# Where the first image's sampling starts in a conv-attention-MLP kernel, the queue of the feed-forward's row loads, and the order of the attention's pools

## The chip, the cores and the metric

The kernel runs on one core of a Trainium2 chip. The engines are TensorE (PE), VectorE (DVE), ScalarE (ACT), GpSimd (POOL) and SyncE (SP, which here only issues DMAs); ACT and POOL issue DMAs too, each in the order of its own instruction stream. Working data lies in SBUF (128 partitions), matmul results in PSUM. The metric is the device time of one execution in microseconds, taken as the median over several executions; lower is better.

## The reference

The input is four images of 64 x 64 positions with 256 channels in 32-bit floats, and everything stays in that type. Two layers follow each other. Cut to what matters:

```python
# layer 0, per image; xn is the group-normalised image
xp = xn @ in_w + in_b
x1 = silu(batchnorm(depthwise_conv3x3(xn)))
offset = x1 @ off_w + off_b                  # 8 groups x 9 points x (x, y), per position
mask = softmax(x1 @ mask_w + mask_b)         # over the 9 points
out = sum over the 9 points of mask * bilinear_sample(pad(xp), grid + offset)
x = x + (out @ out_w + out_b)
# layer 1, per image of 4096 tokens; t = x
n1 = layernorm(t); q = n1 @ Wt; k = n1 @ Wx.T
a = softmax_over_k( tanh(q[:, None] + k[None, :] + bh) @ Wa + ba )      # 32 units
t = t + a @ n1
n2 = layernorm(t); w = n2 @ wr + br
idx = the 2047 tokens with the largest w
t = t + scatter(idx, (gelu(n2[idx] @ w1 + b1) @ w2 + b2) * w[idx]) + n2
```

## The kernel before, in words

**Offsets and weights.** `offsets_and_weights` is a generator over four images of eight slabs each (a slab is 512 tokens, four tiles of 128). Each slab normalises, convolves on PE and DVE, makes offsets and masks, and turns them into weights over a 5 x 5 window of the projected image; these go to DRAM (`wt`), the projected image as well (`xp`), and a table of it for gathers (`tab`). In each slab it can yield at five places, so that other work is put between: before its window, after the first step of the window, and after three more.

**Sampling.** `sample_image(n)` is a generator too. Offsets beyond the window are rare; `list_tokens` makes a list of the tokens that have one, with a chain of small DVE operations and 32 PE matmuls of one-hot columns (L647 to L651), and `exact_rows` computes those tokens exactly with 144 indirect gathers `ga` on POOL (L724). For all others the window sum runs in four chunks of 1024 tokens, two channel halves and 25 window positions: load `wb` (the weight of that position, broadcast over channels, L819), multiply it with the shifted image `xs` (L828), and add to the accumulator `ac` (L838). Each of the two DVE operations is 128 x 1024 elements, and there is a yield behind each. A finished chunk goes through PE (L784) and is written to `t` in DRAM. At its end the exact rows are put over the approximate ones (L762).

**First stage.** All four images' offsets come first, with the sampling of image 0 beside them. In the driver (near L1522) the generator of offsets runs alone through image 0, and then each yield of the 24 slabs of images 1 to 3 is followed by 4, 4, 4, 3 and 3 steps of the sampler, 18 a slab.

**Per image.** The driver then loops over the images. A first scope holds the feed-forward of the image before, the preparation of this image's attention (layer norm, unit products, exponentials to `kf` and through DRAM to `qf`) and steps of the next image's sampling; a string of turns sets the order. A second scope holds the attention with sampling beside it: PE forms `d` from `qf` and `kf` (L1017), ACT takes logarithms into a ring of buffers `r` (pool `rp`, L1111), POOL, DVE and PE multiply them up, and exponentials `et` (pool `ep`) weight the values. The last feed-forward runs alone.

**Feed-forward.** `feed_forward` finds the threshold of the 2047 largest weights, writes each of 32 tiles of rows with an indirect scatter on POOL to its sorted place in DRAM (`sort`, L1423), and then loads four chunks of 512 sorted rows back (`chunk`, L1455, on SP's queue). Each load waits for all 32 scatters. ACT normalises the rows (L1463), PE transposes them (L903), and the two matmuls with gelu follow (`ph` L1483, `py` L1489); the results are scattered to the output on POOL (L1496). `chunk(s + 1)` is called behind the second of the four scatters of chunk s.

**Order.** A planner (the Tile framework) orders each engine's instructions; those wrapped in `keep` or issued through `pinned` stay in program order on their engine, others may be moved. SBUF pools are a stack: a scope's pools take their bytes in the order in which they are named, and a pool that lies on bytes of a closed one waits for all that used the closed pool. In the first scope of an image the order is `one` (53 KB per partition: the feed-forward's buffer `big` and its weights), `two`, `sb`, `row`, `rp`. In the attention it is `two`, `sb` (15 KB together), `rp` (24 KB), `qp` (16 KB, the queries `qf` and `qn`), `ep` (34 KB), `ap`.

Of the kernel before, what the change touches and what calls it, by code (L numbers as in the profile page):

```python
# [18 lines left out]
NB, H, W, C = 4, 64, 64, 256  # L19
L = H * W  # L20
NT = L // P
# [8 lines left out]
SLAB = 8  # L30
# [7 lines left out]
PVB = 8  # L38
# [8 lines left out]
def layers_kernel(ctx: ExitStack, tc: tile.TileContext, a, out: bass.AP):  # L47
    nc = tc.nc
# [183 lines left out]

    S = SimpleNamespace(bank=True, wants=False, gather=True, left=0, tables=[])

    def bank_taken():
        S.wants = not S.bank
# [28 lines left out]
    def offsets_and_weights(images, slab, rows_bufs):  # L267
# [300 lines left out]
        ns = NT // slab  # L568
# [4 lines left out]
        for i in range(len(images) * ns):  # L573
            at, s = divmod(i, ns)
            if s == 0:
                cur = ahead
                after = front(images[at + 1]) if at + 1 < len(images) else {}
            one, two, three, four = after.get(s, nothing)
            cur.taps(s)
            one()  # L580
            if s + 1 < ns:
                cur.convolution(s + 1)
            elif at + 1 < len(images):
                ahead = image(at + 1)
                ahead.convolution(0)
            if at:
                yield
            window = cur.window(s)
            three()
            next(window)  # L590
            if at:
                yield
            two()
            if s % 2 == 0:
                rows16 = cur.projection(s // 2)
                next(rows16)
            else:
                next(rows16, None)
            if last:
                last[0].turn(last[1])  # L600
            last = cur, s
            for _ in range(3):
                next(window)
                if at:
                    yield
            four()
            if at == 0 and s == ns - 1:
                yield
        last[0].turn(last[1])

    def positions(fl, vec):
# [154 lines left out]
    def sample_image(n, sums=1):  # L766

        S.left = STEPS
        uf = yield from list_tokens(n)
        yield
        exact = []
        single = exact_rows(n, uf, exact)

        def matmuls(c, ac, i):
            g = c * (CH // P) + i
            xr = S.sb.tile([P, 2, C], F32, tag="xr", name="xr")
            nc.sync.dma_start(out=xr, in_=x_d[n, g * P : (g + 2) * P].rearrange("(t p) c -> p t c", p=P))  # L780
            pm = S.ps_m.tile([P, 2, C], F32, tag="pm", name="pmo")
            for j in range(2):
                for k in range(CC):
                    nc.tensor.matmul(  # L784
                        pm[:, j, :], ac[:, k, rows(i + j)], outwp[:, k, :],
                        start=(k == 0), stop=(k == CC - 1),
                    )
            keep(nc.gpsimd.tensor_add(  # L788
                xr, xr, outb.rearrange("p (o c) -> p o c", o=1).to_broadcast([P, 2, C])
            ))  # L790

            def add():
                (nc.vector if sums == 1 else pinned).tensor_add(xr, pm, xr)
                nc.sync.dma_start(
                    out=t_d[n][g * P : (g + 2) * P].rearrange("(t p) c -> p t c", p=P), in_=xr
                )

            return add

        late, adds = [], []  # L800

        def outputs():

            while adds:
                adds.pop(0)()
            for _ in range(min(2, len(late))):
                adds.append(late.pop(0)())

        for c in range(L // CH):
            ac = S.dn.tile([P, CC, CH], F32, tag="ac", name="ac", bufs=sums)  # L810
            for f in range(CC):
                xs = S.dn.tile([P, CH // W + 4, MP], F32, tag="xs2", name="xs2")
                o = c * (CH // W) * MP
                nc.sync.dma_start(
                    out=xs.rearrange("p r w -> p (r w)"), in_=xp_d[n][f, :, o : o + (CH // W + 4) * MP]
                )
                for d in range(ND):
                    wb = S.dn.tile([P, CH], F32, tag="wb", name="wb", bufs=2)
                    nc.sync.dma_start(  # L819
                        out=wb, in_=wt_d[n][f, d : GH * ND : ND, c * CH : (c + 1) * CH].partition_broadcast(CG)  # L820
                    )
                    src = xs[:, d % WIN : d % WIN + CH // W, d // WIN : d // WIN + W]
                    if d == 0:
                        pr = ac[:, f, :]
                    else:
                        prt = S.dn.tile([P, CH], F32, tag="prd", name="prd")
                        pr = prt
                    keep(nc.vector.tensor_tensor(  # L828
                        pr.rearrange("p (r w) -> p r w", w=W), src, wb.rearrange("p (r w) -> p r w", w=W),
                        ALU.mult,  # L830
                    ))
                    S.left -= 1
                    if d % 8 == 2:
                        outputs()
                    own = S.gather and next(single, None)
                    yield
                    if d > 0:
                        keep(nc.vector.tensor_add(ac[:, f, :], ac[:, f, :], pr))  # L838
                        S.left -= 1
                        yield  # L840
                    while own:
                        own = next(single, None)
                        S.left -= 1
                        yield
            if sums > 1:
                late = [functools.partial(matmuls, c, ac, i) for i in range(0, CH // P, 2)]
                continue
            for i in range(0, CH // P, 2):
                while bank_taken():
                    yield  # L850
                matmuls(c, ac, i)()
                S.left -= 1
                yield
        while late or adds:
            outputs()
            yield
        for _ in single:
            S.left -= 1
            yield
        put_rows(n, *exact[0])  # L860
        S.left = 0
# [505 lines left out]
    def feed_forward(n, vec):  # L1367
# [40 lines left out]
        sl, _ = positions(eq, vec)  # L1408
# [3 lines left out]
        sl, _ = positions(gt, vec)  # L1412
# [36 lines left out]
        def chunk(s):  # L1449

            o = nh + s % 2 * nx
            xs = big[:, o : o + nx].rearrange("p (t c) -> p t c", t=4)
            o = nh + 2 * nx + s % 2 * nv
            vs = big[:, o : o + nv].rearrange("p (t c) -> p t c", t=4)
            get = nc.sync.dma_start(  # L1455
                out=xs, in_=sort_d[n][s * 512 : (s + 1) * 512].rearrange("(t p) c -> p t c", p=P)
            )
            for ins in put:
                tc.add_manual_dep(get.ins, ins.name, in_order, reason="rows in order")
            si = S.two.tile([P, 4], I32, tag="si", name="si")  # L1460
            vec.tensor_scalar(si, xs[:, :, C + 3], float(n * L), None, ALU.add)
            for t in range(4):
                nc.scalar.activation(  # L1463
                    vs[:, t, :], xs[:, t, :C], AF.Identity, bias=xs[:, t, C + 1 : C + 2], scale=xs[:, t, C : C + 1]
                )
            xT = S.row.tile([P, CC, 512], F32, tag="vT", name="xT")
            transpose4(xT, vs, vec)

            nc.gpsimd.tensor_tensor(vs, vs, xs[:, :, :C], ALU.add)
            for t in range(4):  # L1470
                vec.scalar_tensor_tensor(
                    vs[:, t, :], b2, xs[:, t, C + 2 : C + 3], vs[:, t, :], ALU.mult, ALU.add
                )
            held[s] = xs, vs, si, xT
# [43 lines left out]
    with scope(  # L1518
        ("a_one", 1, 0), ("a_xn", 2, 0), ("a_ld", 2, 0), ("a_wk", 2, 0), ("a_w1p", 1, 0), ("a_sm", 2, 0),
        ("smp", 2, 0), ("two", 2, 0), ("sb", 2, 0), ("dn", 1, 0), ("a_t", 3, 1), ("a_m", 3, 1), ("ps_m", 2, 1),  # L1520
    ):
        others = offsets_and_weights(range(NB), SLAB // 2, 1)  # L1522
        next(others)
        first = sample_image(0, 2)
        for at, _ in enumerate(others):
            for _ in range((4, 4, 4, 3, 3)[at % 5]):
                next(first, None)
        for _ in first:
            pass
    sample_any(0)  # L1530
    for n in range(NB):
        with scope(("att", 1, 0), ("smp", 2, 0), ("dn", 1, 0)):
# [24 lines left out]
                        pass  # L1557
            S.gather = True
            with scope(
                ("two", 2, 0), ("sb", 2, 0), ("rp", 6, 0), ("qp", 2, 0),  # L1560
                ("ep", 2 * PVB + 1, 0), ("ap", 1, 0), ("ps_d", 2, 1), ("ps_n", 3, 1), ("ps_m", 1, 1),
            ):
                attention(n, v, kf, [sampling])
        attention_any(n)
# [41 lines left out]
```

## Time and profile before

| | us |
|---|---|
| median of three executions | 10425.71 (10424.51 to 10445.72) |
| the profiled execution, its span | 10430.83, 10429.1 |
| PE, DVE, ACT, POOL busy in the span | 9290.6, 8530.2, 7464.3, 5220.7 |
| first stage: offsets of all images beside sampling of image 0 | 0 to 1361 |
| preparation and attention of image 0 | 1361 to 1470, to 3465 |
| feed-forward 0 with preparation 1, attention 1 | 3465 to 3850, to 5765 |
| feed-forward 1 with preparation 2, attention 2 | 5765 to 6150, to 8060 |
| feed-forward 2 with preparation 3, attention 3 | 8060 to 8373, to 10130 |
| feed-forward 3, alone | 10130 to 10429 |

The boundaries are read from the starts of token loads, query loads and last matmuls on the timeline. Shares of the whole span say little here: attention, which the change touches only at its start, is three quarters of it. So the stretches in question are cut out by their start and end, and the busy and idle time of each engine in a stretch is compared with the stretch. A timeline line gives start, duration, engine, source line, operation, tile written from tiles read, shape, count, and in brackets the idle time of the engine before it with what ended that.

### The profile page before, as it was taken

What the parts mean: (1) busy time and instruction counts of PE and PEld (TensorE: products, weight loads), DVE (VectorE), ACT (ScalarE), POOL (GpSimd) and SP (SyncE); (2) the same over time, 40 slices, a digit from 0 to 9 for tenths busy, and PEclk for the clock granted to TensorE, in tenths of its full rate; (3) what the DMA queues carried; (4) which work ended last, traced back from release to release, by engine and by line L of the source; (5) the groups of instructions that cost most, each with busy time, mean ns of one, the idle gap of its engine ahead of it and who ended that gap; (6) DMA issues with size and microseconds to landing.
All of it is one profiled execution on the core that took longest, in us unless ns stands there. A gap on an engine that the chain in (4) does not pass through costs nothing. (4 is left out here: it accounts for less than half of the span.)

```text
span 10429.1 us, 117382 instructions
## 1 busy us (share of the span) xinstructions
PE 9290.6 (89%) x38892; PEld 4512.6 (43%) x38892; DVE 8530.2 (82%) x13743; ACT 7464.3 (72%) x8525; POOL 5220.7 (50%) x3042
## 2 busy tenths in 40 slices
PE   5777779999999589999999589999999699999995
PEld 3444434444444344444444344444444344444443
DVE  5788979898989679899898689899898367777772
ACT  3333348887888438888888358888887389999991
POOL 0231027776555327676655247677555155555552
PEclk8788879999999789999999789999999799999997
DMA  3466642222222342112111442122111300000002
GB/s 104 137 200 192 200 129 64 62 65 60 72 66 72 121 151 54 52 53 56 53 58 44 139 137 54 53 51 56 52 58 38 103 13 8 10 7 7 7 5 76
DMA packets 381591, 766.07 MB, mean 73 GB/s; under 512 B 49360, under 2 KB 212848, under 8 KB 380944
## 3 DMA queue, kind: packets, MB, share of 16 engines
q1 hardware_dynamic: 290448, 608.84, 18.3%
q0 software_dynamic: 30144, 45.87, 3.0%
q10 hardware_dynamic: 60352, 103.50, 2.8%
q8 instruction: 312, 5.11, 0.2%
q14 instruction: 335, 2.74, 0.1%
HBM read 580.88 MB, written 177.14 MB: 73 GB/s over the span
## 5 line engine op out<-in xcount | busy, mean ns | idle before, releaser
L1032 DVE TENSOR_TENSOR r<-nn,r 128x512 f32<-128x512 f32 x6144 | 3942.2, 683 | 865.7 <-PE nn L1027 807.4
L1027 PE MATMUL nn<-qn,kf 32*128 32x512 f32 (+1 forms) x12288 | 4518.4, 640 | 134.5 <-DVE r L1032 97.5
L1117 POOL TENSOR_TENSOR r<-r 128x1024 f32<-128x1024 f32 x1024 | 2708.2, 2645 | 2645.1 <-DVE r L1032 2633.0
L1111 ACT ACTIVATE r<-d 128x1024 f32<-128x1024 f32 x3072 | 3114.2, 1014 | 1093.4 <-DVE r L1121 688.8
L1017 PE MATMUL d<-qf,kf 32*128 32x512 f32 (+1 forms) x12288 | 3338.7, 632 | 77.3 <-DMA qf<-qf 42.9
L1113 ACT ACTIVATE r<-r 128x1024 f32<-128x1024 f32 x3072 | 3124.1, 1051 | 32.7
L1027 PEld LDWEIGHTS nn<-qn,kf 32*128 32x128 f32 (+1 forms) x12288 | 1400.3, 185 | 1900.0 <-DVE r L1032 1452.4
L1055 PE MATMUL pv<-v,et 128*128 128x257 f32 x8192 | 2110.6, 401 | 14.9 <-DVE acv L1079 14.9
L1055 PEld LDWEIGHTS pv<-v,et 128*128 128x128 f32 x8192 | 1511.6, 194 | 979.0 <-issue 770.7
L1017 PEld LDWEIGHTS d<-qf,kf 32*128 32x128 f32 (+1 forms) x12288 | 1017.7, 186 | 1340.0 <-issue 734.0
L1119 POOL TENSOR_TENSOR r<-r 128x512 f32<-128x512 f32 x1024 | 1330.5, 1299 | 98.3 <-DVE r L1032 23.1
L828 DVE TENSOR_TENSOR prd<-xs,wb 128x1024 f32<-128x1024 f32 x768 | 983.6, 1281 | 79.2 <-DMA wb<-wt 71.4
L838 DVE TENSOR_TENSOR ac<-ac,prd 128x1024 f32<-128x1024 f32 x768 | 990.9, 1290 | 6.6
L724 POOL DMA_INDIRECT ga<-tab,tii x576 | 698.6, 1213 | 353.8 <-DVE so L738 208.6
L1039 ACT ACTIVATE et<-et,nshift 128x512 f32<-128x512 f32 x1024 | 723.5, 707 | 29.7 <-DVE et L1124 29.7
L1121 DVE TENSOR_TENSOR r<-r 128x512 f32<-128x512 f32 x1024 | 720.3, 703 | 4.1 <-POOL r L1117 3.7
L1124 DVE TENSOR_TENSOR et<-r 128x512 f32<-128x512 f32 x1024 | 697.4, 681 | 0.4
L263 PE MATMUL pc<-xn,diag 128*128 128x512 f32 x1008 | 452.2, 604 | 21.7 <-ACT xn L397 8.3
L788 POOL TENSOR_TENSOR xr<-xr,outb 128x512 f32<-128x512 f32 x64 | 88.1, 1381 | 551.4 <-DMA xr<-in_x_dram 486.1
L263 PE MATMUL ptc<-ident,xp 128*128 128x128 f32 (+1 forms) x576 | 136.9, 352 | 207.3 <-ACT tb L456 204.9
L263 PEld LDWEIGHTS pc<-xn,diag 128*128 128x128 f32 x1008 | 191.7, 193 | 257.2 <-issue 223.6
L456 ACT COPY tb<-ptc 128x256 f32<-128x256 f32 (+1 forms) x288 | 104.5, 370 | 240.7 <-PE ptc L263 132.4
(342 smaller groups left out, 5251.9 us busy)
## 6 DMA issues: line engine op xcount, KB each, us to landing
wb<-wt SPq DMA_DIRECT2D x800, 512.0 KB
tab<-tb ACTq DMA_DIRECT2D x128, 256.0 KB
v<-t SPq DMA_DIRECT2D x64, 512.0 KB
xs<-xp SPq DMA_DIRECT2D x32, 680.0 KB
xp<-xp ACTq DMA_DIRECT2D x32, 544.0 KB
xt<-in_x_dram SPq DMA_DIRECT2D x32, 512.0 KB
xr<-in_x_dram SPq DMA_DIRECT2D x64, 256.0 KB
t<-xr SPq DMA_DIRECT2D x64, 256.0 KB
```

What stands on the lines that cost most here:

```text
L263: return lambda *args, **kw: keep(op(*args, **kw))
L828: keep(nc.vector.tensor_tensor(pr.rearrange("p (r w) -> p r w", w=W), src, wb.rearrange("p (r w) -> p r w", w=W), ALU.mult,))
L838: keep(nc.vector.tensor_add(ac[:, f, :], ac[:, f, :], pr))
L1017: keep(nc.tensor.matmul(d[:, j, :], kf[g, blk, rows(kt)], qs[q][0][g, blk, :], start=True, stop=True))
L1027: keep(nc.tensor.matmul(nn, kf[g, blk, rows(kt)], qs[q][1][g, blk, :], start=True, stop=True))
L1032: keep(nc.vector.tensor_tensor(r[:, j, :], ns[j], r[:, j, :], ALU.mult))
L1039: keep(nc.scalar.activation(ets[b], ets[b], AF.Exp, bias=nshift))
L1055: keep(nc.tensor.matmul(pv, ets[b0 + i][:, rows(j)], v[:, k0 + i, :], start=(i == 0), stop=(i == PVB - 1)))
L1111: keep(nc.scalar.activation(rs[b, p], ds.pop((b, p)), AF.Ln))
L1113: keep(nc.scalar.activation(rs[b, p], rs[b, p], AF.Exp, scale=-1.0))
L1117: keep(nc.gpsimd.tensor_tensor(rs[b, 1], rs[b, 1], rs[b, 2], ALU.add))
L1119: keep(nc.gpsimd.tensor_tensor(rs[b, 1][:, 0], rs[b, 1][:, 0], rs[b, 3][:, 0], ALU.add))
```

## The change

Several things are changed. The generator of offsets yields from the fifth slab of the first image on (it yielded only from the second image on), and yields its slab number, 0 to 31. The driver puts 3, 3, 2, 2 and 2 steps of the sampler into slabs 4 to 7 and 4, 4, 3, 3 and 3 into each later one. The list of far tokens, which needs the offsets of the whole image, is made by the sampler at its first multiply at or after slab 9 and no longer as its first act; later images list first, as before. The four row loads of a feed-forward go from SP's queue to POOL's. In the attention's scope `ep` takes the place of `rp` and `qp`, behind it come `rp`, `ap` and `qp`.

```diff
-    S = SimpleNamespace(bank=True, wants=False, gather=True, left=0, tables=[])
+    S = SimpleNamespace(bank=True, wants=False, gather=True, left=0, tables=[], listing=True)
...
-            if at:
-                yield
+            if i >= ns // 2:
+                yield i
             window = cur.window(s)
             three()
             next(window)
-            if at:
-                yield
+            if i >= ns // 2:
+                yield i
...
             for _ in range(3):
                 next(window)
-                if at:
-                    yield
+                if i >= ns // 2:
+                    yield i
             four()
-            if at == 0 and s == ns - 1:
-                yield
...
         S.left = STEPS
-        uf = yield from list_tokens(n)
-        yield
-        exact = []
-        single = exact_rows(n, uf, exact)
+        exact, single = [], None
+        if S.listing:
+            uf = yield from list_tokens(n)
+            yield
+            single = exact_rows(n, uf, exact)
...
                     if d % 8 == 2:
                         outputs()
+                    if single is None and S.listing:
+                        uf = yield from list_tokens(n)
+                        yield
+                        single = exact_rows(n, uf, exact)
                     own = S.gather and next(single, None)
...
-            get = nc.sync.dma_start(
+            get = nc.gpsimd.dma_start(
                 out=xs, in_=sort_d[n][s * 512 : (s + 1) * 512].rearrange("(t p) c -> p t c", p=P)
             )
...
-        others = offsets_and_weights(range(NB), SLAB // 2, 1)
-        next(others)
+        slabs = NT * 2 // SLAB
+        S.listing = S.gather = False
         first = sample_image(0, 2)
-        for at, _ in enumerate(others):
-            for _ in range((4, 4, 4, 3, 3)[at % 5]):
+        for at, i in enumerate(offsets_and_weights(range(NB), SLAB // 2, 1)):
+            if i == slabs + 1:
+                S.listing = S.gather = True
+
+            for _ in range((3, 3, 2, 2, 2)[at % 5] if i < slabs else (4, 4, 3, 3, 3)[at % 5]):
                 next(first, None)
...
-                ("two", 2, 0), ("sb", 2, 0), ("rp", 6, 0), ("qp", 2, 0),
-                ("ep", 2 * PVB + 1, 0), ("ap", 1, 0), ("ps_d", 2, 1), ("ps_n", 3, 1), ("ps_m", 1, 1),
+                ("two", 2, 0), ("sb", 2, 0), ("ep", 2 * PVB + 1, 0), ("rp", 6, 0), ("ap", 1, 0), ("qp", 2, 0),
+                ("ps_d", 2, 1), ("ps_n", 3, 1), ("ps_m", 1, 1),
```

## The prediction

> **What bounds the kernel now.** The page's 40 slices come first. PE holds 9 in the long attention stretches; the first three and a half slices (the offsets of all images beside the first image's sampling) are lower on PE and higher on DVE.
>
> ```profile
> PE   5777779999999589999999589999999699999995
> DVE  5788979898989679899898689899898367777772
> PEclk8788879999999789999999789999999799999997
> ```
>
> The change touches that first stage, three overlaps of a feed-forward with the next attention's preparation, and the last feed-forward. Next I cut the first stage at the window-weight clears that open slabs 4, 7, 8 and 31, and asked each stretch for its busy time. Columns: window, length, then busy us and count for PE, PE loads, DVE, ACT, POOL, then clock, DMA share, GB/s.
>
> ```profile
> 251.90:335.70 83.80, 64.67 (x210) 40.14 (x209) 54.88 (x115) 45.70 (x71) 1.14 (x8) 0.82 0.28 100
> 335.70:403.10 67.40, 54.67 (x194) 35.84 (x193) 34.25 (x101) 18.11 (x29) 7.74 (x8) 0.77 0.25 71
> 403.10:1338.40 935.30, 699.95 (x2170) 395.33 (x2168) 849.59 (x1163) 321.69 (x541) 175.63 (x161) 0.84 0.63 197
> 1338.40:1361.50 23.10, 13.13 (x60) 10.45 (x60) 12.69 (x26) 4.84 (x12) 3.82 (x3) 0.72 0.42 133
> ```
>
> Slabs 8 to 30 take 935.3/23 = 40.67 us each and DVE is busy for 849.59 of 935.30: DVE bounds them, with 85.7/23 = 3.7 us idle a slab. Slabs 4 to 6 take 27.9 us each with DVE idle for 28.9 us in all, and the step from slab 7 to slab 8 leaves it idle for another 33.1. Tile by tile, the sampling is an equal pair of DVE operations that begins only there, although its operands were loaded long before:
>
> ```profile
> L828 DVE TENSOR_TENSOR prd<-xs,wb x206: 1160/1224/3487, 399.2 to 1496.5; 128x1024 f32<-128x1024 f32 x103
> L838 DVE TENSOR_TENSOR ac<-ac,prd x205: 1159/1224/2299, 400.5 to 1483.2; 128x1024 f32<-128x1024 f32 x103
> L819 SPq DMA_DIRECT2D wb<-wt x217: 512/513/619, 212.3 to 1498.8; - x109
> ```
>
> The last lines are from the timeline (start, duration, engine, line, in brackets the idle time before and who ended it). At 381 us DVE makes the list of far tokens and stands 15.1 us for PE's matmuls of it. At 3589 to 3631 the row loads of the first feed-forward stand at the head of SP's queue until the scatters have landed; wb loads for the sampling stand behind them.
>
> ```profile
> 381.22 0.87 DVE L647 TENSOR_TENSOR oh<-slotr,bf 128x256 f32<-128x256 f32 x2 [15.08 <-PE pl L651]
> ...
> 3605.48 1.22 DVE L838 TENSOR_TENSOR ac<-ac,prd 128x1024 f32<-128x1024 f32 x1
> ...
> 3623.01 0.96 POOL L1423 DMA_INDIRECT sort<-v,rif  x1 [0.30 <-DMA sort<-v,rif]
> 3625.77 0.37 SPq L1455 DMA_DIRECT2D big<-sort  x1
> 3626.25 0.52 SPq L819 DMA_DIRECT2D wb<-wt  x1
> ...
> 3629.41 2.07 ACT L1463 ACTIVATE big<-big 128x256 f32<-128x256 f32 x4 [25.10 <-DMA big<-sort]
> 3631.11 1.23 DVE L828 TENSOR_TENSOR prd<-xs,wb 128x1024 f32<-128x1024 f32 x1 [24.41 <-DMA wb<-wt]
> ```
>
> Durations are from one execution of 10430.8 us (span 10429.1), 5.1 above the median of 10425.7; savings are taken off the median.
>
> **Part A, the sampling begun in slab 4.** Nothing is removed: 48 steps of the sampler (four slabs of 3+3+2+2+2) move into slabs 4 to 7, and later slabs take 17 steps instead of 18. A step is one DVE operation of 1.22 us, so 48 x 1.23 = 59 us of DVE work arrives where DVE was idle for 28.9 + 33.1 = 62.0 us. Not all the idle time can be filled. Slabs 4 to 6 become DVE bound: 54.88/3 = 18.3 us of own work plus 12 x 1.23 = 14.8, plus the 3.7 us that such a slab leaves idle, is 36.8 instead of 27.9. They lengthen by 27 us in all, and the sampling that leaves slabs 8 onward pays it back. I count the stage by DVE's idle time, since its busy time, 951.4 us from 251.9 to 1361.5, stays. Idle before: 28.9 + 33.1 + 85.7 + 10.4 (the tail after 1338.4) = 158.2. After: slabs 4 to 6, 3 x 3.7 = 11; the step from 7 to 8, 10 (its 33.1 less the list's 15.1 and less a part that samples fill); slabs 8 to 30 the same 85.7; the list, now in slab 9 among full DVE work, 12 (its 15.1 with a little in front of it); the tail 10.4. Sum 129, a gain of 29 us. The list's own DVE and PE work is moved only. Bounds: nothing, if the first image's chain through PE and ACT lengthens by as much as is inserted; 47, if the list hides entirely and slab 7 is as tight as the others (158.2 - 4 x 3.7 - 85.7 - 10.4). Moved DMAs: 48 steps carry some 25 wb loads of 0.51 us on SP and the xs loads, which in before sit prefetched from 212.3 on; in slabs 4 to 7 the DMA share is 0.25 to 0.28 against 0.63 later, so they are hidden. The 144 gathers on POOL move later by about a slab; POOL is busy for 176 of 935 us and hides them. With 408 + 48 steps against about 423 the sampler ends in slab 30 instead of 31, so its closing matmuls and row writes overlap the last windows; this is inside the 10.4 of tail.
>
> **Part B, the order of pools in the attention.** SBUF is a stack; a new pool waits for everything that used its bytes. The query buffers lay on the feed-forward's bytes and move to bytes that are free early; the exponent ring of six (rp) instead moves onto the feed-forward's, the preparation's small pool (two) and its row pool. At the third transition the queries wait for the last scatter:
>
> ```profile
> 8373.24 1.22 SPq L1000 DMA_DIRECT2D qf<-qf  x2
> ...
> 8379.59 1.94 ACT L1111 ACTIVATE r<-d 128x1024 f32<-128x1024 f32 x2 [28.84 <-PE d L1017]
> ```
>
> ACT writes rp there, so the earliest start is when the scatter has landed, 8373.3: a gain of 6.3 us. At the first two transitions rp would wait instead for the last reader of `two`, the cast of `wide` on DVE (3856.58, behind a wait of 16.8 us for rows of x), while the first Ln ran at 3854.37: a loss of 2.3, and 2.0 by the same rows of the second. Net gain 2; bounds -4 (no gain at the third) and +18 (the cast does not hold rp, and all three start with the scatter's landing, at the first 3848.2 against 3854.37).
>
> **Part C, row loads on POOL's queue.** Removed: 16 loads at 0.36 to 0.58 us of SP. Added: 16 on POOL. SP no longer stands from 3596 to 3625, so wb loads go on; but DVE keeps program order and has only some seven operations (8 us) before the minimum over PE's product at 3638.8, which needs ACT's exponent, and ACT itself stands for the rows until 3629. Gain 0 to 8 at each of two overlaps (the third has no sampling), taken 4: 8 us. Cost: the trace has no plain load on POOL. One indirect scatter of 128 rows takes 0.96 us: as one instruction the load would cost as much, by count of its 512 rows 3.8. Against SP's 0.46 the first load of a feed-forward, on its path, costs 0.5 to 3.4 us more; I take 2 (no row favours an end) at each of four: 8. The other twelve cost nothing, because chunk 2's rows land by 10334.2 and are first used by PE's transposes near 10349.8; without that cover they cost 4 to 7 each (rival 2). What is queued behind a waiting load on POOL is the next chunk's addition, 2.35 us, which waits for the same rows anyway. Net 0, bounds -14 (0 less 4 x 3.4) to +14 (16 less 4 x 0.5).
>
> The Trainium skill, "SBUF — State Buffer", section "SBUF: two separate sides", speaks against part C: GpSimd writes descriptors itself and can be held up while DVE runs certain fast copies, about 620 against 3100 ns. By that the four first loads could cost about 2.5 us more each, 10 in all. The scatters here took 0.96 us while DVE stood and up to 1.96 beside its work, so the trace shows the direction and less of the size.
>
> Sum: 29 + 2 + 0 = 31; 10425.7 - 31 = 10395 (10400 on the profiled execution's own time).
>
> **Rivals.**
> 1. The first image is a chain. Slabs 4 to 7 lengthen by what is inserted, and only the list changes place: A is 0, time 10424. For it: PE is busy for 64.7 of 83.8 us there and waits for ACT. Against: 62 us of DVE idle.
> 2. Slower, by one mechanism: POOL's stream keeps each next chunk's load where the code has it, behind the chunk's second scatter. That scatter ends at 10324.6 in the last feed-forward; landing 2.4 (the shortest of the row DMAs), ACT 2.1, transposes 2.8 and copy 1.2 give xT at 10333.1 or later, where PE began the next chunk at 10329.1: 4 us, or 7 with a 3.8 us load, for each of 12 chunks, 48 to 84. Taken 60: 10455. It decides from 31/12 = 2.6 us a chunk. Against it: the SP loads of chunks 0 and 1 go out together, and on POOL chunk 1's addition (3687.23) stands ahead of chunk 0's first scatter (3694.39), so the planner does move such work ahead of code order.
> 3. C pays fully: ACT's order shifts too and both overlaps gain their whole 24.4 and 25.4 us, 42 more than counted: 10353. Against it: ACT waits for the rows themselves.
>
> **How the numbers follow.** Forecast .50 (own range 10378 to 10414: A between 47 and 10), rival 1 .17, rival 2 .20, rival 3 .13. Leaving out the outer part of rivals 2 and 3 gives 10362 to 10450. A measurement tells about 0.2%, 20.9 us, from no change: below 10404.8 lies most of the forecast and rival 3, .55; between lies rival 1 and a part of the forecast and of 2, .25; above 10446.6 most of rival 2 and some unknown, .20.
>
> **What would show it.** Right: sampling on DVE from about 255 us; slabs 4 to 6 near 37 us; a list stall near 450; the stage's token loads at about 1330; at 3590 no wb wait of 24 us but a wait for PE or ACT; loads on POOL's queue beside the first scatters landing; the first Ln of image 3 some 6 us sooner after the last scatter. Wrong: slabs 8 to 30 still at 40.7 us with the stage's end unmoved, or chunks of the last feed-forward further apart than the 28.4 us of now.

## The result and the profile after

The changed kernel takes 10424.3 us against 10440.1 us for the kernel before, run beside it: a ratio of 0.9987 (95% interval 0.9980 to 0.9993), some 14 us less (7 to 21). The forecast was 31 us less. By the bound of 0.2% this is the case "within", which had been given a chance of 25%. The forecast was counted from a median of 10425.7, which the longer series puts at 10440. So the raw time lies outside the forecast's own range (10378 to 10414) and inside the wide one (10362 to 10450), and it meets the 10424 of rival 1 by luck: 14 us off the old median would be some 10412. The profiled execution of the changed kernel took 10422.3 us (span 10420.5).

The stages, each from one profiled execution. "Overlap" is a feed-forward with the next attention's preparation, from its first token load to the first logarithm of the attention.

| stage, us | before | after | difference | forecast |
|---|---|---|---|---|
| first stage, to its token load | 1361.5 | 1344.3 | -17.2 | -29 |
| preparation 0 | 109.8 | 110.2 | +0.4 | 0 |
| overlap 1 | 360.7 | 371.1 | +10.4 | +2 by B, -2 by C |
| overlap 2 | 362.6 | 375.0 | +12.4 | +2 by B, -2 by C |
| overlap 3 | 288.5 | 283.0 | -5.5 | -6 by B, +2 by C |
| attentions 0 to 3, sum | 7714.2 | 7705.7 | -8.5 | 0 |
| last feed-forward | 231.9 | 231.2 | -0.7 | +2 |

The first stage, in the same view as before (window, length, busy us and count of PE, PE loads, DVE, ACT, POOL, then clock, DMA share, GB/s). The windows are slabs 4 to 6, the step from 7 to 8, slabs 8 to 28, and slabs 29 to 31:

```profile
258.24:367.39 109.15, 74.71 (x239) 44.27 (x237) 97.40 (x153) 48.33 (x74) 1.16 (x8) 0.81 0.48 163
367.39:404.25 36.86, 31.09 (x107) 18.50 (x107) 33.18 (x66) 13.87 (x24) 0.00 (x0) 0.86 0.59 189
404.25:1255.30 851.05, 668.43 (x2093) 386.58 (x2091) 752.94 (x1085) 302.74 (x502) 183.48 (x168) 0.84 0.63 193
1255.30:1344.30 89.00, 55.09 (x190) 36.19 (x190) 50.21 (x94) 26.94 (x52) 3.50 (x3) 0.75 0.32 109
```

The same last three slabs of the kernel before:

```profile
1264.90:1361.50 96.60, 52.85 (x186) 34.24 (x184) 82.38 (x121) 22.94 (x46) 3.82 (x3) 0.75 0.51 168
```

Slabs 4 to 6 now take 36.4 us each and slab 7 takes 36.9 instead of 67.4: the sampler fills them as forecast. But DVE, idle for 14.2 of the last 96.6 us before, is idle for 38.8 of the last 89.0 after. The sampler has run out of work in slab 29, and the last offsets stand alone as a chain again. Much of the idle time was moved from the beginning of the stage to its end.

The whole stage in the same columns, before and after:

```profile
0.00:1361.50 1361.50, 973.56 (x3094) 568.07 (x3094) 1098.04 (x1750) 477.32 (x787) 203.53 (x229) 0.83 0.53 166
0.00:1344.30 1344.30, 972.54 (x3094) 572.71 (x3094) 1087.49 (x1750) 480.31 (x788) 203.35 (x229) 0.83 0.54 168
```

DVE runs the same 1750 instructions. It is idle for 263.5 us before and 256.8 after, so only 6.7 of the 17.2 us are idle time; its busy time fell by 10.5.

In the sampling's tiles, the multiply begins at 249.6 instead of 399.2:

```profile
L827 DVE TENSOR_TENSOR prd<-xs,wb x207: 1159/1224/2300, 249.6 to 1493.7; 128x1024 f32<-128x1024 f32 x104
L841 DVE TENSOR_TENSOR ac<-ac,prd x207: 1160/1224/2174, 250.9 to 1499.1; 128x1024 f32<-128x1024 f32 x104
```

Then the timeline of the first overlap after the change (start, duration, engine, line, operation, and in brackets the idle time before and who ended it):

```profile
3584.84 1.22 DVE L827 TENSOR_TENSOR prd<-xs,wb 128x1024 f32<-128x1024 f32 x1
...
3602.99 1.60 POOL L1458 DMA_DIRECT2D big<-sort  x2 [2.18 <-DMA sort<-v,rif]
...
3607.15 2.08 ACT L1466 ACTIVATE big<-big 128x256 f32<-128x256 f32 x4 [33.53 <-DMA big<-sort]
...
3610.18 3.78 PE L953 MATMUL pk<-mm,sel 64*128 64x512 f32 x4 [32.03 <-ACT qe L961]
...
3615.05 1.23 DVE L263 TENSOR_REDUCE least<-pk 128x1 f32<-128x1024 f32 x1 [28.99 <-ACT kf L954]
```

No wait for window weights of 24 us is left, as forecast. DVE went on for seven more operations, to 3586, and then stood 29.0 us for the unit's exponential; PE stood 32.0 us where it had stood 20.6, and ACT 33.5 where it had stood 25.1. One long stall on DVE was exchanged for another. PE's line before:

```profile
3633.14 2.89 PE L950 MATMUL pk<-mm,sel 64*128 64x512 f32 x3 [20.58 <-DVE mm L263]
```

The transitions, with the last output scatter, the cast of `wide` and the first logarithm. First overlap, then third:

```profile
3820.98 2.57 POOL L1499 DMA_INDIRECT out_dram<-big,si  x1 [4.49 <-DMA out_dram<-big,si]
...
3839.50 0.14 DVE L263 CAST wide<-lo 1x1 int32<-1x1 f32 x1
...
3839.88 1.94 ACT L1114 ACTIVATE r<-d 128x1024 f32<-128x1024 f32 x2 [58.62 <-DMA tr<-t]
...
8357.58 2.55 POOL L1499 DMA_INDIRECT out_dram<-big,si  x1 [2.40 <-DVE lo L263]
...
8368.70 1.94 ACT L1114 ACTIVATE r<-d 128x1024 f32<-128x1024 f32 x2 [23.01 <-DMA out_dram<-big,si]
```

The same before, first overlap and then the third's last scatter (its logarithm, at 8379.59, stands in the prediction):

```profile
3837.95 2.55 POOL L1496 DMA_INDIRECT out_dram<-big,si  x1 [4.43 <-DMA out_dram<-big,si]
...
3854.37 1.94 ACT L1111 ACTIVATE r<-d 128x1024 f32<-128x1024 f32 x2 [53.47 <-PE d L1017]
...
3856.58 0.14 DVE L263 CAST wide<-lo 1x1 int32<-1x1 f32 x1
...
8361.67 2.55 POOL L1496 DMA_INDIRECT out_dram<-big,si  x1 [2.52 <-DVE lsm L263]
```

From scatter to logarithm it takes 18.9 us at the first (16.4 before), where the logarithm now follows the end of the cast by 0.2 us, and 11.1 us at the third (17.9 before). In all seven executions with the new order of pools the logarithm follows the cast's end by 0.2 to 0.5 us at the first two transitions; in all four with the old order it starts 1.6 to 2.9 us ahead of the cast's end.

### The profile page after: what moved, and what is told of

It reads as the page before. It is cut to its first block, busy times and chain, and to the rows that moved or that the text cites. A ratio compares the mean times of both kernels' runs of the same rounds, so it can differ in the third digit from the quotient of the medians.

```text
span 10420.5 us, 117367 instructions
## 1 busy us (share of the span) xinstructions
PE 9281.3 (89%) x38892; PEld 4511.9 (43%) x38892; DVE 8523.7 (82%) x13743; ACT 7466.9 (72%) x8526; POOL 5246.2 (50%) x3058
## 3 DMA queue, kind: packets, MB, share of 16 engines
q1 hardware_dynamic: 282000, 600.32, 17.8%
## 5 line engine op out<-in xcount | busy, mean ns | idle before, releaser
L1426 POOL DMA_INDIRECT sort<-v,rif x128 | 133.2, 1040 | 291.6 <-DVE rif L263 176.2
```

## The experiments

After this reading I held that part A gives 17 us and loses the rest at the stage's end, and that part C costs some 10 us in each of the first two overlaps. The first four runs test both, and a way to make C pay. Ratios are against the kernel before, with their 95% intervals.

### e1: row loads back on SP

```diff
-            get = nc.gpsimd.dma_start(
+            get = nc.sync.dma_start(
```

> The changed kernel with the row loads back on SP's queue. Stages are measured from the first token load of an overlap (feed-forward with the next preparation) to the first logarithm of its attention: 360.8, 362.6 and 288.5 us before, 371.1, 375.0 and 283.0 changed. My theory: part C makes the first two longer, by 4 us of later rows (the 32 scatters take 45.4 instead of 42.2 us beside more DVE work) and 4 us of matmuls at half clock behind a longer PE stall. Then both return to about 361 to 364, the third stays at 283, and the time falls by some 20 us. Rival: the pool order (part B) or the sampler's other position (part A) makes them longer. Then they stay at 371 to 375 and the time stays.

Measured: ratio 0.9989 (0.9980 to 0.9999), 10431 us. The overlaps took 370.8, 363.4 and 282.5 us. The second fell by 11.6, the first not at all, and the time did not fall. The 20 us expected did not come.

### e2: only the row loads on POOL

```diff
# in the kernel before
-            get = nc.sync.dma_start(
+            get = nc.gpsimd.dma_start(
```

> The kernel before with the row loads on POOL's queue and nothing else changed. My theory: the first two overlaps go from 360.8 and 362.6 to about 369 and 373, the third and the last feed-forward stay within 1 us, the first stage ends at 1361 as before; the time rises by 15 to 20 us. Rival (parts A and B cause the longer overlaps): 361 and 363, no change of time.

Measured: ratio 1.0006 (0.9996 to 1.0016), 6 us more with an interval that holds zero. Overlaps 368.2, 364.7 and 292.9 us. The third, where no change was expected, rose by 4.4. With e1 this says that C costs between nothing and some 10 us in all. My theory of 20 us finds no support: it had been read from one pair of executions.

### e0: the changed kernel again

> The changed kernel once more, beside the runs that follow. First token load at 1344 to 1352, overlaps (first token load to first logarithm) 371 and 372 plus or minus 5, 283 plus or minus 5 for the third. If the length of a preparation is set by how many of its matmuls run at half clock, about 0.5 us each, the spread between executions of the same code follows that count; the rival, that it is fixed by the code, expects the same length again within 1 us.

Measured: ratio 0.9992 (0.9983 to 1.0001). First token load 1338.1, 6 us earlier than the expected 1344 to 1352; overlaps 366.9, 367.8 and 283.0 us, so 4 and 7 us shorter than in the first execution of the same code. The preparation of image 0, which no part of the change edits, shows what varies. Three executions of it, of e2, of the changed kernel and of e3:

```profile
1360.60:1467.20 106.60, 74.90 (x238) 39.71 (x238) 80.88 (x185) 36.84 (x54) 4.87 (x5) 0.79 0.52 173
```

```profile
1344.30:1454.40 110.10, 79.31 (x238) 41.12 (x238) 81.24 (x185) 36.82 (x53) 4.56 (x5) 0.73 0.49 167
```

```profile
1319.10:1438.70 119.60, 87.71 (x238) 44.20 (x238) 81.23 (x185) 36.88 (x53) 5.41 (x5) 0.69 0.45 153
```

The counts of instructions agree, DVE's and ACT's busy time too; PE's goes from 74.9 to 87.7 us as its granted clock goes from 0.79 to 0.69. Counted on the timeline, 3, 13 and 29 of the 96 unit products (128x512 or 64x512, most of 0.59 us) ran for more than 0.8 us, most of these for 1.06. Over eleven executions the length follows that count: 3 give 106.5, 12 and 13 give 110, 19 and 20 give 111.4 and 113.4, 26 to 29 give 116.4 to 119.6, about 0.5 us for each.

### e3: sixteen steps a slab

```diff
-            for _ in range((3, 3, 2, 2, 2)[at % 5] if i < slabs else (4, 4, 3, 3, 3)[at % 5]):
+            for _ in range((3, 3, 2, 2, 2)[at % 5] if i < slabs else (4, 3, 3, 3, 3)[at % 5]):
```

> The changed kernel with 4, 3, 3, 3, 3 steps (16) in each slab from the eighth on, instead of 17: 432 steps for a sampler of some 423. My theory: the sampler runs dry in slab 29 of the changed kernel and leaves DVE idle for 38.9 us in slabs 29 to 31, of which before had 14.5; with 16 it ends in slab 30 or 31, the stage's first token load comes at about 1325 instead of 1344, and the time falls by 15 to 20 us. Rival: the offsets of the last images are a chain through PE and ACT that needs its time anyway; idle time only moves to earlier slabs, and the token load stays within 5 us of 1344.

Measured: token load at 1319.2, ratio 0.9979 (0.9968 to 0.9991). Slabs 8 to 28 and 29 to 31:

```profile
401.30:1230.40 829.10, 659.57 (x2088) 384.69 (x2087) 729.77 (x1064) 302.13 (x500) 179.31 (x168) 0.85 0.63 192
1230.40:1319.17 88.77, 57.80 (x199) 37.38 (x197) 77.17 (x116) 28.21 (x54) 3.65 (x3) 0.79 0.53 174
```

DVE is idle for 11.6 us in the last three slabs, not 38.8, and slabs 8 to 28 are 22 us shorter. The loss at the end of the stage is thereby shown: the sampler had been given its 423 steps too early. The rival, that the offsets' own chain needs the time, falls. Of the 25 us, preparation 0 took 9 back in this execution, as half clock. The whole time gained less than expected: by the ratios it is some 8 us below the changed kernel, within their intervals, where 15 to 20 were expected. The overlaps took 369.6, 372.8 and 292.5 us, the last 9.5 more than in the changed kernel, which has the same code there. What the steps are worth in the whole time shows better between e4 and e7 below.

### e4: the units' exponentials ahead of the loaded rows

```diff
+                norm = nc.scalar.activation(
...
+                for unit in units:
+                    tc.add_manual_dep(norm.ins, unit.ins.name, in_order, reason="units first")
...
+        units = S.tables[-1:]
         chunk(0)
...
-                        "mos" + "m" * 3 + "mo" * 8 + "om" + "oss" * 2 + "m" + "oss" * 7 + "m" + "oss" * 3
+                        "mos" + "m" * 3 + "mo" * 8 + "om" + "oss" * 2 + "m" + "oss" * 10 + "m"
```

> The changed kernel, loads on POOL's queue, but ACT's normalisation of the loaded rows ordered behind the exponentials of the preparation's units traced so far, and the first chunk called three preparation turns later. My theory: in part C the freed SP queue gains nothing only because ACT stands for the rows with the units' exponentials behind it, so PE stands 32 us and DVE 29 us. With the order changed both work on while the scatters land, and the first two overlaps fall from 371 and 375 to about 350 (20 us or more each); time 40 us less. Rival: the chunks' chain behind the rows, 215 us long, sets the end whatever is done earlier, and they fall by 5 us or less.

Measured: ratio 0.9964 (0.9950 to 0.9978), 10408 us. Overlaps 352.9 and 350.5 us, 14 to 24 us below those of the changed kernel. ACT in the first overlap:

```profile
3603.08 1.02 ACT L954 ACTIVATE kf<-pk 128x1024 f32<-128x1024 f32 x1 [4.58 <-PE pk L953]
3608.12 1.02 ACT L961 ACTIVATE qe<-pf 128x1024 f32<-128x1024 f32 x1 [4.01 <-DVE prd L827]
3611.22 1.02 ACT L954 ACTIVATE kf<-pk 128x1024 f32<-128x1024 f32 x1 [2.07 <-PE pk L953]
3618.11 1.02 ACT L961 ACTIVATE qe<-pf 128x1024 f32<-128x1024 f32 x1 [5.87 <-PE pf L959]
...
3626.32 1.60 POOL L1458 DMA_DIRECT2D big<-sort  x2 [6.45 <-DMA sort<-v,rif]
...
3630.73 4.04 ACT L1466 ACTIVATE big<-big 128x256 f32<-128x256 f32 x8 [11.59 <-DMA big<-sort]
```

The units go on while the scatters land, and ACT stands 11.6 us for the rows where it stood 33.5. The rows are taken later (146.9 us after the overlap's start, 138.4 in the changed kernel) and the overlap ends sooner all the same. The two edits, the order on ACT and the later first chunk, were not separated. The third overlap, which has no sampling to fill with, took 293.1 us, 10 more; its rows were taken 24.7 us behind the last scatter's start instead of 7.8. But e3 had 292.5 with the changed kernel's own order, so this 10 is not clear of the spread between executions.

### e5: the same order with SP's queue

The edit of e4, made in the kernel before.

> The kernel before, loads on SP's queue, with the same order as e4 (rows' normalisation behind the units, first chunk three turns later). My theory: DVE needs the window weights that stand behind the row load on SP's queue, so the order alone is worth little: overlaps of 357 and 359 against 360.8 and 362.6, 8 us at most in all. Rival: the order on ACT alone brought e4's gain and the queue is indifferent; then they fall to about 345, 15 us or more each.

Measured: ratio 0.9989 (0.9980 to 0.9999), overlaps 367.7, 363.0 and 278.1 us. The first two gained nothing; DVE stood 25.9 us for window weights in the first, and the rows, now ordered behind the units, were taken only 34 us after the last scatter. The 11 us in the time may be the third overlap's 10, but the profiled execution was itself the slowest of ten, so this is not shown; why this order would suit the third with loads on SP and not (e4) on POOL was not followed up.

### e6: the pools in their old order

```diff
-                ("two", 2, 0), ("sb", 2, 0), ("ep", 2 * PVB + 1, 0), ("rp", 6, 0), ("ap", 1, 0), ("qp", 2, 0),
-                ("ps_d", 2, 1), ("ps_n", 3, 1), ("ps_m", 1, 1),
+                ("two", 2, 0), ("sb", 2, 0), ("rp", 6, 0), ("qp", 2, 0),
+                ("ep", 2 * PVB + 1, 0), ("ap", 1, 0), ("ps_d", 2, 1), ("ps_n", 3, 1), ("ps_m", 1, 1),
```

> The changed kernel with the attention's pools in their old order (part B undone). My theory: the third transition loses 5 to 6 us (last scatter to first logarithm 17 to 18 us instead of 11), the first two gain 2 us at most (16 to 17 instead of 18 to 19), so the time stays within 5 us. Rival: part B also moves the queries' or the ring's waits inside the attention, and the attentions change by 5 us or more each.

Measured: ratio 0.9989 (0.9980 to 0.9998). Last scatter to first logarithm: 17.2, 17.6 and 18.0 us, against 18.9, 17.7 and 11.1 in the changed kernel (18.2, 17.8 and 10.9 in e0). The third loses 6.8 to 7.1, the first gains 1.0 to 1.7 and the second 0.1 to 0.2. The attentions sum to 7712.0 us, within the 7705.7 to 7723.8 of the runs that share the changed kernel's attention.

### e7 and e8: both repairs, with POOL's and with SP's queue

e7 is the changed kernel with e3's sixteen steps, and e4's order in the first two overlaps only (`units` empty and the old turns for the third). e8 differs from it in one word:

```diff
-            get = nc.gpsimd.dma_start(
+            get = nc.sync.dma_start(
```

> The changed kernel with 16 steps a slab as in e3, and e4's order for the first two overlaps only. My theory: the gains are of different stages and add up: first token load at about 1320, overlaps near 352, 351 and 283 to 288, time some 50 us under before (10390). Rival: what the first stage gains comes back as half clock in the preparation behind it, as e3's 119.6 us there against 110 suggests; then it stays at e4's level, within 10 us of 10408.

> The kernel of e7 with the row loads back on SP's queue. My theory: with the order of e4 the freed SP queue is what lets DVE and PE work on while the scatters land, so without it DVE stands some 25 us for window weights in each of the first two overlaps again, as e5's trace shows, and these go from 358.5 and 354.9 us to about 365; the first token load stays near 1316 and the time rises by 10 to 25 us, to some 10385. Rival: the queue is indifferent and the order alone brought the gain; then overlaps and time stay within 4 us of e7's.

Measured: e7 0.9938 (0.9926 to 0.9950), 10369 us, 65 us below before. e8 0.9963 (0.9951 to 0.9975), 10397 us. In e7 the token load comes at 1313.3 and the overlaps take 358.5, 354.9 and 284.1 us; in e8 1327.6 and 367.5, 368.6 and 282.2. e7 gained more than the 50 us expected, although its first two overlaps are 4 to 7 us longer than expected; against e4 it is some 27 us faster by the ratios, with sixteen steps and the old order in the third overlap. In e8 DVE stands for window weights again, once in each of the first two overlaps, where e7 has no such wait over 1.9 us:

```profile
3604.61 1.22 DVE L827 TENSOR_TENSOR prd<-xs,wb 128x1024 f32<-128x1024 f32 x1 [28.31 <-DMA wb<-wt]
...
5908.28 1.23 DVE L827 TENSOR_TENSOR prd<-xs,wb 128x1024 f32<-128x1024 f32 x1 [28.43 <-DMA wb<-wt]
```

So the queue is worth some 26 us by the ratios (28 by the medians) once ACT's order lets DVE and PE use it, and about nothing before. The first two overlaps hold 22.7 us of it in the profiled executions; the first stage, which the edit does not touch, differs by another 14 there. e7 is the fastest kernel of this study.

## Why the prediction was right or wrong

**Part A, its front: right.** Slabs 4 to 6 were forecast at 36.8 us and took 36.4 in the mean. The step from 7 to 8 was forecast with 10 us idle and had 3.7. The list's price was forecast at 12; DVE's idle time in slabs 8 to 10 rose from 12.9 to 23.7 us, 10.8 more.

**Part A, its end: the step that failed.** It is "slabs 8 to 30 the same 85.7; ... the tail 10.4" with "the sampler ends in slab 30 instead of 31 ... this is inside the 10.4 of tail". Of those terms the last three slabs are 14.2 us of idle time. They measured 38.8: the sampler ended in slab 29, with 8 multiplies and adds there and none in 30, where before it had 17 in slab 30. So "instead of 31" was misread too: before has none in slab 31. I had the numbers for it, 456 steps offered against 423 needed, and 33 spare steps are two slabs without sampling, but I looked only at where the sampler ends and not at who fills DVE after it. 16 steps a slab bring the stage's 25 us back (e3).

**A second term of part A was held fixed without a reason:** "its busy time ... stays". For the same 1750 instructions it fell by 10.5 us, and in the means of three and five executions from 1097.1 to 1087.4. In the records one DVE instruction begins before the one ahead of it ends 542 times before and 622 times after; this overlap makes up most of the fall. So the 17 us came out nearer to the 29 than the idle time alone, 6.7, would have put them.

In means over executions with the same first stage, the token load came at 1360.4 before (three), at 1344.7 with 17 steps (five) and at 1320.0 with 16 (three): gains of 15.7 and 40.4 us, where 29 was forecast for 17 steps. At the first logarithm of image 0, behind the preparation, the means are 1469.7, 1458.1 and 1438.4, so 11.6 and 31.3 us are left; the preparation ran more of its products at half clock (its means are 109.2, 113.5 and 118.3 us). That the earlier start causes the lower clock is only suggested by these means; e1 and e7 had the same 117 us behind first stages 37 us apart.

**Part B: right.** The third transition gained 6.8 us against 6.3, the first lost 2.5 against 2.3, the second 0.7 against 2.0; e6 gives the same directions with the opposite sign. The cause is as forecast: the first logarithm waits for the scatter at the third and for the cast at the first two.

**Part C: the sum near nought, both terms too large.** Forecast was 8 gained and 8 lost. DVE did get seven more operations done, and stopped at the minimum over PE's product, as named. They were worth nothing, since the 29 us stall behind them simply began earlier. The first load costs less than the 2 us that I took: from the last scatter's start to the rows' use it took 7.3, 7.7, 7.8 and 7.7 us against 6.4, 6.6, 6.5 and 6.6, about 1.1 us each, with 0.80 us of POOL per load; e1, with SP's queue, had 6.5 to 8.9, so this price rests on few executions. Together that would be some 4 us lost; measured is -2 (e1 against the changed kernel) to +6 (e2), no more than the intervals. That the sum came near the forecast is luck: a gain and a cost, both taken as 8, shrank together.

The first overlap's 10.4 us split into 2.6 until the rows are taken, 5.3 from there to the last output scatter and 2.5 behind it; in e0 they were 3.3, 1.1 and 1.8, so half of them did not come again.

**Rival 2 (next chunk's load behind the second scatter): did not happen.** POOL issued the loads of chunks 0 and 1 together (the line of 1.60 us) and each later one right behind the fourth scatter of the chunk before last. **Rival 3 (C pays fully when ACT's order shifts too):** named as a rival at 42 us, and it is what e4 and e7 bring about by hand, at some 26 us against e8; in the change itself ACT's order stayed. **Rival 1** was too dark: the first image's slabs are not a pure chain.

As far as the runs resolve it, the measured 14 us thus come from A: 11.6 at the first logarithm, and B and C near zero, where the forecast had 29 and 2. (The lower end of the forecast's own range, 10378, leaves out the 2 us of B that its upper end counts.)

## What to carry to other kernels

When filler work is spread over a stage by a fixed number of steps, check the end as well as the front: an idle stretch filled at the beginning opens at the end if the filler runs out, and a pace that spends the last steps near the stage's end keeps the gain (e3). A freed queue pays only as far as the next in-order engine lets the work through; name that engine and put its blocked instruction behind the work that could run. And a difference of 10 us in one stage of one execution is not a finding until the same code has been seen twice.

## What the runs showed of the hardware

**PE came out of its stalls at half clock, and stayed there for 6 to 16 us of work.** In the first overlap the same sequence of matmuls, changed kernel and kernel before:

```profile
3629.97 3.78 PE L938 MATMUL pq<-vT,wqk 128*128 128x512 f32 x4
3633.68 3.78 PE L959 MATMUL pf<-mm,sel 64*128 64x512 f32 x4
3637.39 5.96 PE L1486 MATMUL ph<-xT,w 128*128 128x512 f32 x8
```

```profile
3652.88 3.78 PE L935 MATMUL pq<-vT,wqk 128*128 128x512 f32 x4
3656.59 1.98 PE L956 MATMUL pf<-mm,sel 64*128 64x512 f32 x4
3658.50 4.99 PE L1483 MATMUL ph<-xT,w 128*128 128x512 f32 x11
```

Four products take 3.78 us at half clock and 1.98 at full. After a gap of 4.9 us before `pk` the kernel before was back at full clock 7.4 us later; the changed one, after a gap of 4.3 us, only 15.7 us later, although PE was busy for 16.14 of the 16.20 us around them:

```profile
3626.20:3642.40 16.20, 16.14 (x19) 5.69 (x20) 11.68 (x14) 4.02 (x4) 0.00 (x0) 0.51 0.38 134
```

The length of the stall ahead does not explain it. Directly behind its stall of 32.0 us the changed kernel was back after 7.9 us, and behind 20.6 us the kernel before after 6.4. What sets the time is not shown. Nor does half clock explain the first overlap's 10 us: nine more products at 1.06 instead of 0.59 us are some 4 us here, but over the whole overlap the changed kernel had fewer of its 96 unit products above 0.8 us (29 against 40), and PE was busy for 226.2 us against 230.3. The Trainium skill, "TensorE: Matmul & The Clock Gate", section "Part 1: The HAM clock gate", says that half rate is the resting state and that about 3.4 us of sustained work release it; the rows agree on the half rate and the release, which took two to five times as long.

**POOL's scatters lengthen beside the sampling's operations on DVE.** The train of 32 scatters, from the first start to the last, took 39.3 us in the last feed-forward, 41.2 in the first overlap before (DVE stopped half way), 44.4 in the changed kernel and 48.1 in e4, where DVE works all through; the longest is 49.5 in e7, 26% more. The instructions are the same. In all eleven executions, 340 of the 1408 row scatters overlapped a 128x1024 multiply or add of the sampling on DVE, and 137 of these took 1.10 to 1.98 us. No other took more than 1.06, whether DVE stood (830) or did other work (238), nor did any of the 127 of these 1068 during which the DMA engines were busy for more than half. So the sampling's DMA traffic alone is not the cause. The warning in the Trainium skill, "SBUF — State Buffer", section "SBUF: two separate sides", names the direction for certain fast copies on DVE, with a factor of five for a single DMA that these runs do not show: here a single scatter at most doubled.
